# A twelve-layer decoder on one core: evacuations, divisions and norms change engines, and the first batch entry gets a queue of its own

## The chip, the cores and the metric

The kernel runs on one core of a Trainium2 chip, in one launch. The metric is the time of one execution in microseconds (us); the median of three runs of the kernel before is 2718.15 us. Engines are named as the profile names them: PE is TensorE (matrix products and transposes), DVE is VectorE, ACT is ScalarE, POOL is GpSimd and SP is SyncE, which issues the DMAs. PEld is the loading of weights into TensorE.

## The reference

The input is x with 4 batch entries, 512 positions and 128 features, and a context of 154 positions for each entry. Four groups of three layers follow, each added to its input and normalised:

```
x = norm(x + L0_attn(x));  x = norm(x + L0_xattn(ctx, x));  x = norm(x + L0_ffn(x))
x = norm(x + L1_attn(x));  x = norm(x + L1_xattn(x, ctx));  x = norm(x + L1_ffn(x))
x = norm(x + L2_attn(x));  x = norm(x + L2_xattn(x, ctx));  x = norm(x + L2_ffn(x))
x = norm(x + L3_attn(x));  x = norm(x + L3_xattn(x, ctx));  x = norm(x + L3_ffn(x))
```

L0_attn and L3_attn are self-attention with 16 heads of 8 features; L0_attn rotates x by position before it projects queries and keys with biases, L3_attn projects x down first. The four xattn layers are attention from the 512 positions to the 154 context positions, again 16 heads of 8; L0_xattn, L1_xattn and L2_xattn have biases on queries and keys, L3_xattn has none. L0_xattn puts the outputs of its heads back in another order and normalises twice, with a scale and an offset (gamma, beta) between. L1_attn is a state-space layer with a recurrence over the positions, L2_attn a causal attention with 16 heads of 64, and the ffn layers are gated or routed networks. All data are float32.

## The kernel before, in words

The order of work on every engine is written out by hand: each engine runs its instructions in the order in which the program emits them. A layer is a generator that yields between pieces, so that the end of a layer may be emitted among the first pieces of the next. An agenda holds small pieces of work for a later step.

**Operands in parts.** A head has only 8 features. To use TensorE's rows, and to keep float32 accuracy with bf16 products, queries and keys are split into three bf16 parts, and the parts are laid out so that one product of 64 rows gives a head's scores. `send` (L403) does this for one batch entry: a projection on TensorE (L407), its evacuation from PSUM to `raw` with scale and bias, on ScalarE where a scaled bias is at hand (L409, L411) and otherwise on VectorE (L413), four operations that cut `raw` into three parts (L414 to L417; cast, subtract, cast, subtract), and six DMAs that write the parts to a scratch in device memory, `far_q`, `far_k` or, for cross-attention, `far_kc` (L421). `arrive` (L479) loads the scratch back in the operands' layout with two DMAs into `qP` or `kP`. `other_rows` writes constant rows of the scratch at the start. The temporary `raw` and the parts come from a room that the layer gives (`room_to_send`), often with one buffer, so a second `send` waits for the first one's DMAs. All these DMAs are issued by SP.

**Maxima.** Scores are computed twice: once to reduce each row's maximum on VectorE, once transposed for the exponential on ScalarE. `split_maxima` (L493 to L496) turns the maxima into bf16 parts on GpSimd, and `link_maxima` turns these over on TensorE (L504) and adds them into rows of the query operand on VectorE (L506), so that the transposed product comes out with the maximum already subtracted.

**Self-attention** (`self_attention`) takes 64 steps, 16 for each batch entry. In a step come two score products (L667) and their maximum (L671) for a head pair six steps ahead, the transposed products (L683) and exponentials (L692) of this step, and the weighted sums (L706) of two steps back. Divisions by the sums, the output projection, the residual sum and the norm of a finished batch entry come from the agenda; `applied` (L344 to L346) is the norm's last operation, once for each of four tiles of 128 positions. In L0_attn `source` gives the rotated input: six operations on GpSimd (L789 to L794) and a transpose on TensorE. At steps 7, 10 and 13 of each 16, `new["room"]` lets the next layer send operands of its own ahead.

**Cross-attention** (`cross_attention`) goes in steps of four heads, 16 in all and two to fill the pipeline. In a step n: the first half of the scores and maxima (L949, L962) of step n+2 and of the transposed products (L957) and exponentials (L968) of step n; the first sums of step n-1 (L990); `link_maxima` for n+1; pieces of the agenda; the second halves; the remaining sums of n-1 (L999); the leftover keys of n (L978); `split_maxima` for n+2. In L0_xattn (`shuffled`) the remaining sums are followed on VectorE by a 32x32 transpose (L1011), a reciprocal (L1013) and the multiplication into `zt` (L1014). After four steps a batch entry's `zt` goes through `inner` (residual sum on GpSimd, L1025, and statistics on VectorE) and `outer` (`applied` on VectorE, then gamma, beta and residual on GpSimd, L1030 to L1032). What was not sent ahead is sent here: operands of entry b+2 after the second step of entry b.

**L2_attn** (`Causal`) normalises its probabilities on GpSimd (L1163), transposes them on TensorE (L1179) and copies them out on VectorE and ScalarE (L1515, L1526). During L1_attn and L2_attn, operands of the following cross-attention are sent.

Of the kernel before, what the change touches and what calls it, by code (L numbers as in the profile page):

```python
# [11 lines left out]
F32 = mybir.dt.float32  # L12
# [9 lines left out]
P = 128  # L22
# [152 lines left out]
def decoder_kernel(ctx: ExitStack, tc: tile.TileContext, x, ctxT, mask1, mask3, packs, offsets, out, layers):  # L175
# [102 lines left out]
    def other_rows(far, what, n):  # L278
        for r in range(2):
            nc.sync.dma_start(far[r, 48:, :, :], flat[:, what : what + 1, :n].to_broadcast([16, 8, n]))  # L280

# [61 lines left out]

    def applied(dst, ys, n, mv, rs):  # L344
        for t in range(n):
            nc.vector.tensor_scalar(  # L346
                dst[:, t, :], ys[:, t, :], mv[:, t, 0:1], rs[:, t : t + 1], ALU.subtract, ALU.mult
            )
# [42 lines left out]

    def scaled(what, scale, pool, name):
        if scale == 1.0:
            return what
        t = pool.tile([P, 1], F32, name=name, bufs=1)
        nc.vector.tensor_scalar(t, what, scale, None, ALU.mult)
        return t


    Q_ROWS, K_ROWS = ((0, 1, 3), (3, 2, 2), (4, 1, 1)), ((2, 1, 3), (1, 4, 2), (0, 1, 1))  # L400
    SLOT = 48

    def send(far, order, w, rhs, scale, bias, raw, part, scaled_bias=None, on=nc.gpsimd):  # L403

        n = rhs.shape[-1]
        pj = psum_t("ps_proj", kind="a" if "a" in ring else "t")
        nc.tensor.matmul(pj[:, :n], lhsT=w, rhs=rhs, start=True, stop=True)  # L407
        if bias is None:
            nc.scalar.activation(raw, pj[:, :n], AF.Copy, scale=scale)  # L409
        elif scaled_bias is not None:  # L410
            nc.scalar.activation(raw, pj[:, :n], AF.Identity, bias=scaled_bias, scale=scale)  # L411
        else:
            nc.vector.tensor_scalar(raw, pj[:, :n], bias, scale, ALU.add, ALU.mult)  # L413
        on.tensor_copy(part[:, 0, :], raw)  # L414
        on.tensor_tensor(raw, raw, part[:, 0, :], ALU.subtract)
        on.tensor_copy(part[:, 1, :], raw)
        on.tensor_tensor(part[:, 2, :], raw, part[:, 1, :], ALU.subtract)  # L417
        for i, (at, by, m) in enumerate(order):
            for r in range(2):
                rows = far[r].rearrange("(s k) p c -> (k p) s c", k=DK)  # L420
                nc.sync.dma_start(  # L421
                    rows[:, at : at + by * (m - 1) + 1 : by, :],
                    part[64 * r : 64 * r + 64, i : i + 1, :].to_broadcast([64, m, n]),
                )
# [41 lines left out]
    class Operands:  # L466
# [11 lines left out]

        def arrive(self, dst, far):  # L479

            for p in (slice(0, 2), slice(2, 8)):
                nc.sync.dma_start(dst[:, p, :], far.rearrange("r q p c -> (r q) p c")[:, p, :])

# [40 lines left out]

    def out_pieces(b, o, w, keep, cur, new, last, split=False):

        oT = keep.tile([P, S], F32, tag="oT", name="oT", bufs=1)
        ys = keep.tile([P, NT, D], F32, tag="ys", name="ys", bufs=1)
        xb = []

        def turn_over():
            pt = psum_a("ptO")
            for t in range(NT):
                nc.tensor.transpose(pt[:, t * P : (t + 1) * P], o[:, t].rearrange("p h d -> p (h d)"), ident)
            nc.scalar.copy(oT, pt)
            if "bo" in w:
                xb.append(with_bias(b, w["bo"], keep, cur))
            else:
                xb.append(cur["x"][:, b * NT : (b + 1) * NT, :])

        def times():
            yp = psum_a("yp")
            for t in range(NT):
                nc.tensor.matmul(
                    yp[:, t * P : (t + 1) * P], lhsT=oT[:, t * P : (t + 1) * P], rhs=w["wo"], start=True, stop=True
                )
            nc.vector.tensor_tensor(ys, yp.rearrange("p (t d) -> p t d", t=NT), xb[0], ALU.add)

        return [turn_over, times] + finish_pieces(b, ys, new, last, split)

    def finish_pieces(b, ys, new, last, split=False):
        xs = new["x"][:, b * NT : (b + 1) * NT, :]
        stats = []

        def norm():
            if split:
                applied(xs, ys, NT, *stats)
            else:
                normed(xs, ys, NT, "f")
            if last:  # L560
                nc.sync.dma_start(out[b].rearrange("(t p) d -> p t d", p=P), xs)
# [43 lines left out]
    def self_attention(w, source, q_scale, k_scale, room, keep, pool, cur, new, last):  # L605
# [4 lines left out]
        LEAD, LAG = 6, 2  # L610
        bqs = scaled(w["bq"], q_scale, pool, "bqs") if "bq" in w else None
        ops = Operands(pool, S, 2)
# [4 lines left out]
        def prepare(b):  # L617
# [21 lines left out]
            def queries():  # L639
                far = far_q[cur["index"] % 2][b]  # L640
                if ("q", b) not in cur["sent"]:
                    send(far, Q_ROWS, w["wq"], src, q_scale, bqs, *room_to_send(pool, S), scaled_bias=bqs)
                ops.arrive(m["q"], far)

            def keys():
                if ("k", b) not in cur["sent"]:

                    on = nc.vector if cur["index"] == 0 and b == 0 else nc.gpsimd
                    send(
                        far_k[b], K_ROWS, w["wk"], src, k_scale, w.get("bk"), *room_to_send(pool, S),  # L650
                        scaled_bias=w.get("bk"), on=on,
                    )
                ops.arrive(m["k"], far_k[b])
# [43 lines left out]
        def sums(s, h):  # L697
# [17 lines left out]
            if kt == NT - 1:  # L715
# [3 lines left out]
                if j == 3:  # L719
                    pieces = out_pieces(b, m["o"], w, keep, cur, new, last, split=True)  # L720
                    gaps = (2, 5, 6, 7, 10) if b < B - 1 else range(1, 6)
# [39 lines left out]
        for s in range(steps + LAG):  # L761
# [5 lines left out]

            new["room"] = (lambda n: room_to_send(pool, n)) if s % 16 in (7, 10, 13) else None
            yield PIECE
# [5 lines left out]
    def l0_attn(w, cur, new, last, room):  # L775
# [5 lines left out]
        def source(b):  # L781
# [4 lines left out]

            def turned():
                tmp = pool.tile([P, 2, NT, half], F32, tag="tmp", name="tmp", bufs=1)
                nc.gpsimd.tensor_tensor(rx[:, :, :half], x1, cos, ALU.mult)  # L789
                nc.gpsimd.tensor_tensor(rx[:, :, half:], x1, sin, ALU.mult)  # L790
                nc.gpsimd.tensor_tensor(tmp[:, 0], x2, sin, ALU.mult)
                nc.gpsimd.tensor_tensor(tmp[:, 1], x2, cos, ALU.mult)
                nc.gpsimd.tensor_tensor(rx[:, :, :half], rx[:, :, :half], tmp[:, 0], ALU.subtract)
                nc.gpsimd.tensor_tensor(rx[:, :, half:], rx[:, :, half:], tmp[:, 1], ALU.add)  # L794

# [19 lines left out]
    def cross_attention(w, cur, new, last, room, scale, mask=None, shuffled=False):  # L815
# [179 lines left out]
        def more_sums(n):  # L995
# [7 lines left out]
            if not shuffled:  # L1003
# [9 lines left out]
            nc.vector.reciprocal(rec, ot[:, :, DK])  # L1013
            nc.vector.tensor_tensor(  # L1014
                m["zt"][:, j, :].rearrange("p (s d) -> p s d", d=DK), ot[:, :, :DK],
                rec[:, :, None].to_broadcast([P, 16, DK]), ALU.mult,
            )
            if j == 3:
# [9 lines left out]
                def outer():  # L1028
                    applied(ys, zt, NT, *stats)
                    nc.gpsimd.tensor_tensor(ys, ys, w["gamma"][:, None, :].to_broadcast([P, NT, D]), ALU.mult)  # L1030
# [1374 lines left out]
```

## Time and profile before

| what | us |
|---|---|
| median of three runs (2717.45 to 2719.22) | 2718.15 |
| the profiled execution | 2717.01 |
| its span | 2715.2 |
| TensorE busy | 2445.9 |
| VectorE busy | 1705.6 |
| ScalarE busy | 1240.4 |
| GpSimd busy | 1043.7 |

The span is the time from the first to the last instruction of the profiled execution. Busy time counts instructions at work; a busy TensorE is not TensorE at its peak, since ends of matmuls are modelled. The stages that the change touches lie as follows in the span: the start of L0_attn from 0 to 33 us, its steps to 247, L0_xattn from 247 to some 368, the scans of L1_attn up to 842, L1_xattn from 850 to 1000, L2_attn around 1495 to 1850, L2_xattn from 1890 to 1970, L3_attn from 2100 to 2307, and L3_xattn after it.

In a timeline a line begins with the start and the duration of a group of like instructions in us, then engine, line of the program, operation, the tile written and those read, the shapes and the count. Square brackets give the idle time of the engine just before, and what ended it. "SPq" is SP's issuing of a DMA, not its transfer.

### The profile page before, as it was taken

How to read it: one execution, taken by the hardware profiler on the slowest of the kernel's cores; microseconds unless marked ns; L12 is line 12 of the kernel's file. 1: busy time of each engine (PE TensorE's matmuls, PEld its weight loads, DVE VectorE, ACT ScalarE, POOL GpSimd, SP SyncE). 2: the span in 40 equal slices, each digit the busy share in tenths (PEclk: the TensorE clock that was granted, in tenths of full speed). 3: DMA queues.
4: the chain of work that ended last, by engine and by line, in shares of the span. 5: the costliest groups of instructions: out<-in, count | busy, mean ns of one | idle time of the engine just before them, and what ended most of it. 6: DMA issues, size and time to landing. Idle time of an engine off the chain costs nothing. (4 is left out here: it accounts for less than half of the span.)

```text
span 2715.2 us, 37944 instructions
## 1 busy us (share of the span) xinstructions
PE 2445.9 (90%) x14378; PEld 1182.6 (44%) x14378; DVE 1705.6 (63%) x2931; ACT 1240.4 (46%) x2509; POOL 1043.7 (38%) x1360
## 2 busy tenths in 40 slices
PE   4897889978877989999999999998988999899998
PEld 1333334433334444444444555554455233446665
DVE  5896951289987665555545555556756887664444
ACT  2775432377642434333233555553543777343221
POOL 3332420167665327555542444443445332320000
PEclk9999999989988999999999999998987899999999
DMA  4422210000002400000000000002102241300000
GB/s 136 133 78 90 69 35 0 0 0 0 1 15 73 148 7 0 1 1 1 1 1 1 15 7 7 13 13 83 39 1 59 75 115 25 129 32 0 5 4 8
DMA packets 75558, 96.39 MB, mean 36 GB/s; under 512 B 23664, under 2 KB 62320, under 8 KB 75376
## 3 DMA queue, kind: packets, MB, share of 16 engines
q1 hardware_dynamic: 75376, 93.98, 11.8%
q8 instruction: 113, 1.85, 0.3%
q14 instruction: 69, 0.57, 0.1%
HBM read 63.92 MB, written 33.49 MB: 36 GB/s over the span
## 5 line engine op out<-in xcount | busy, mean ns | idle before, releaser
L1163 POOL TENSOR_TENSOR pr<-pr,zs 128x1024 f32<-128x1024 f32 x192 | 237.1, 1252 | 235.2 <-DVE zs L1160 204.8
L671 DVE TENSOR_REDUCE top<-sc 128x2 f32<-128x1024 f32 x256 | 300.9, 1215 | 37.7 <-PE sc L667 34.6
L692 ACT ACTIVATE pT<-st 128x512 f32<-128x512 f32 x512 | 275.9, 597 | 97.9 <-PE st L683 95.2
L1154 ACT ACTIVATE pr<-scc,nm 128x256 f32<-128x256 f32 (+3 forms) x384 | 198.3, 526 | 175.0 <-DVE nm L1148 107.0
L1148 DVE TENSOR_REDUCE nm<-scc 128x2 f32<-128x1024 f32 x192 | 153.6, 820 | 155.2 <-PE scc L1136 154.0
L962 DVE TENSOR_REDUCE top<-scx 128x4 f32<-128x616 f32 x256 | 192.1, 793 | 80.3 <-PE scx L949 77.3
L968 ACT ACTIVATE pTx<-stx 128x512 f32<-128x512 f32 x256 | 139.4, 596 | 206.8 <-PE scx L949 140.0
L2136 POOL TENSOR_TENSOR hh<-hh,cs 128x1024 f32<-128x1024 f32 x64 | 149.2, 2353 | 84.5 <-DVE hh L2132 61.0
L1287 DVE TENSOR_TENSOR vtmp<-psve,gm 128x1024 f32<-128x1024 f32 x64 | 78.3, 1224 | 153.0 <-PE psve L1282 59.6
L706 PE MATMUL av<-pT,vbuf 128*32 128x256 f32 x2048 | 162.6, 392 | 7.2 <-ACT avs L510 7.2
L493 POOL CAST nmP<-top 128x16 bf16<-128x16 f32 x96 | 25.8, 268 | 372.7 <-DVE top L962 214.3
L337 POOL TENSOR_TENSOR rsf<-mvf,eps 128x4 f32<-128x4 f32 x48 | 9.8, 204 | 392.8 <-DVE mvf L335 391.9
L1130 PE MATMUL scc<-k,q 64*128 64x512 f32 (+3 forms) x768 | 143.4, 471 | 6.7 <-ACT pr L1154 2.9
L2132 DVE TENSOR_TENSOR_SCAN hh<-da,pb 128x1024 f32<-128x1024 f32 x64 | 142.6, 2269 | 0.0
L1179 PE MATMUL ptc<-ident,pr 128*128 128x128 f32 x960 | 136.8, 280 | 5.7 <-POOL pr L1163 4.1
L667 PE MATMUL sc<-kP,qP 64*128 64x512 bf16 x512 | 106.2, 413 | 37.6 <-DMA kP<-far_k 18.9
L1292 POOL TENSOR_TENSOR vtmp<-vtmp 128x512 f32<-128x512 f32 x60 | 76.2, 1269 | 162.3 <-DVE vtmp L1287 137.8
L2145 PE MATMUL acc<-hh,ident 128*128 128x512 f32 x256 | 134.4, 652 | 1.9 <-DVE yt L2154 1.9
L1282 PE MATMUL psve<-w_L_ffn,xT 128*128 128x512 f32 x256 | 122.7, 603 | 14.4 <-ACT pr L1154 11.2
L1192 PE MATMUL avc<-pT,v 128*64 128x512 f32 (+3 forms) x768 | 131.4, 449 | 0.5 <-DVE pT L1515 0.5
L1325 PE MATMUL yT<-gT,w_L_ffn 128*128 128x512 f32 x256 | 123.2, 604 | 0.0
L1179 PEld LDWEIGHTS ptc<-ident,pr 128*128 128x128 f32 x960 | 103.4, 141 | 44.4 <-issue 26.0
(408 smaller groups left out, 5050.3 us busy)
## 6 DMA issues: line engine op xcount, KB each, us to landing
qP<-far_q SPq DMA_DIRECT2D x24, 768.0 KB, 6.1
w_L_ffn<-in_L_ffn SPq DMA_DIRECT2D x24, 512.0 KB, 8.5
far_q<-part SPq DMA_DIRECT2D x44, 192.0 KB, 2.8
qP<-far_q SPq DMA_DIRECT2D x24, 256.0 KB, 3.8
kP<-far_k SPq DMA_DIRECT2D x8, 768.0 KB, 5.8
far_q<-part SPq DMA_DIRECT2D x44, 128.0 KB, 2.4
kP<-far_kc SPq DMA_DIRECT2D x16, 231.0 KB, 4.8
w_L_attn<-in_L_attn SPq DMA_DIRECT2D x6, 512.0 KB, 6.5
```

The costliest lines, as they stand in the source:

```text
L671: return lambda: nc.vector.tensor_reduce(top[:, qt, 2 * gp : 2 * gp + 2], sc, AX.X, ALU.max, negate=True)
L692: nc.scalar.activation(pT, st, AF.Exp)
L706: nc.tensor.matmul(m["av"][32 * g : 32 * g + 32, part], lhsT=m["v"][:, kt, 4 * j + g, :], rhs=weights_of[s, g][:, part], start=(kt == 0 an ...
L962: nc.vector.tensor_reduce(ops.maxima(a)[:, 2 * qp : 2 * qp + 2, 2 * gp : 2 * gp + 2].rearrange("p i r -> p r i"), sc, AX.X, ALU.max, negat ...
L968: nc.scalar.activation(pT, st, AF.Exp)
L1130: nc.tensor.matmul(sc[:, r, at : at + n], lhsT=q[rows, qt * P : n], rhs=k[rows, :n], start=(i == 0), stop=False, skip_group_check=True,)
L1148: nc.vector.tensor_reduce(nm[:, i, :], sc[:, :, at : at + (qt + 1) * P], AX.X, ALU.max, negate=True)
L1154: nc.scalar.activation(pr[:, r, at:to], sc[:, r, at:to], AF.Exp, bias=nm[:, i, r : r + 1], accum_out=zs[:, i, r : r + 1],)
L1163: nc.gpsimd.tensor_tensor(pr[:, :, at : at + n], pr[:, :, at : at + n], zs[:, i, :, None].to_broadcast([P, 2, n]), ALU.mult)
L1179: nc.tensor.transpose(pt[:, r, to : to + P], self.pr[u, p][:, r, lo : lo + P], ident)
L2132: nc.vector.tensor_tensor_scan(flat, das[g % 2][:, c].rearrange("p n t -> p (n t)"), pbs[c].rearrange("p n t -> p (n t)"), 0.0, ALU.mult, ...
L2136: nc.gpsimd.tensor_tensor(m["h", j][c], m["h", j][c], m["C", j], ALU.mult)
```

## The change

- In `send`, the evacuation of every biased projection is a ScalarE activation. Where the scale isn't 1, one small VectorE operation scales the bias first. VectorE's evacuation (L413) is gone.
- For the first batch entry of L0_attn, the rotation and the split of the queries are on VectorE; the keys' `send` and `arrive` are issued from ScalarE's queue, and their temporaries come from a pool of their own, `first`.
- The norm's `applied` is on GpSimd for the first three batch entries of L0_attn and L3_attn, and in `outer` of L0_xattn.
- The multiplication into `zt` in L0_xattn is on GpSimd.
- `new["room"]` is given only up to step 59, so that the sends of step 61 come later, in the cross-attention after its second step.
- The order of the parts in the operands (`Q_ROWS`, `K_ROWS`, `SLOT`) is another one, of the same sizes.

```diff
@@ other_rows
-            nc.sync.dma_start(far[r, 48:, :, :], flat[:, what : what + 1, :n].to_broadcast([16, 8, n]))
+            nc.sync.dma_start(far[r, 32:48, :, :], flat[:, what : what + 1, :n].to_broadcast([16, 8, n]))
@@ applied
-    def applied(dst, ys, n, mv, rs):
+    def applied(dst, ys, n, mv, rs, on=nc.vector):
         for t in range(n):
-            nc.vector.tensor_scalar(
+            on.tensor_scalar(
                 dst[:, t, :], ys[:, t, :], mv[:, t, 0:1], rs[:, t : t + 1], ALU.subtract, ALU.mult
             )
@@ send
-    Q_ROWS, K_ROWS = ((0, 1, 3), (3, 2, 2), (4, 1, 1)), ((2, 1, 3), (1, 4, 2), (0, 1, 1))
-    SLOT = 48
-
-    def send(far, order, w, rhs, scale, bias, raw, part, scaled_bias=None, on=nc.gpsimd):
+    Q_ROWS, K_ROWS = ((1, 1, 3), (6, 1, 2), (0, 1, 1)), ((0, 3, 3), (1, 6, 2), (2, 1, 1))
+    SLOT = 32
+
+    def send(far, order, w, rhs, scale, bias, raw, part, on=nc.gpsimd, by=nc.sync):
...
-        elif scaled_bias is not None:
-            nc.scalar.activation(raw, pj[:, :n], AF.Identity, bias=scaled_bias, scale=scale)
         else:
-            nc.vector.tensor_scalar(raw, pj[:, :n], bias, scale, ALU.add, ALU.mult)
+            if scale != 1.0:
+                scaled_bias = small.tile([P, 1], F32, tag="sb", name="sb", bufs=2)
+                nc.vector.tensor_scalar(scaled_bias, bias, scale, None, ALU.mult)
+                bias = scaled_bias
+            nc.scalar.activation(raw, pj[:, :n], AF.Identity, bias=bias, scale=scale)
...
-                nc.sync.dma_start(
+                by.dma_start(
@@ arrive
-        def arrive(self, dst, far):
+        def arrive(self, dst, far, by=nc.sync):
...
-                nc.sync.dma_start(dst[:, p, :], far.rearrange("r q p c -> (r q) p c")[:, p, :])
+                by.dma_start(dst[:, p, :], far.rearrange("r q p c -> (r q) p c")[:, p, :])
@@ out_pieces and finish_pieces hand `on` through
-                applied(xs, ys, NT, *stats)
+                applied(xs, ys, NT, *stats, on=on)
@@ self_attention
-                    send(far, Q_ROWS, w["wq"], src, q_scale, bqs, *room_to_send(pool, S), scaled_bias=bqs)
+                    on = nc.vector if cur["index"] == 0 and b == 0 else nc.gpsimd
+                    send(far, Q_ROWS, w["wq"], src, q_scale, w.get("bq"), *room_to_send(pool, S), on=on)
...
             def keys():
+                if cur["index"] == 0 and b == 0:
+
+                    with tc.tile_pool(name="first", bufs=1, side="right") as first:
+                        send(
+                            far_k[b], K_ROWS, w["wk"], src, k_scale, w.get("bk"), *room_to_send(first, S),
+                            on=nc.vector, by=nc.scalar,
+                        )
+                    ops.arrive(m["k"], far_k[b], by=nc.scalar)
+                    return
...
-                    pieces = out_pieces(b, m["o"], w, keep, cur, new, last, split=True)
+                    on = nc.gpsimd if b < B - 1 else nc.vector
+                    pieces = out_pieces(b, m["o"], w, keep, cur, new, last, split=True, on=on)
...
-            new["room"] = (lambda n: room_to_send(pool, n)) if s % 16 in (7, 10, 13) else None
+            new["room"] = (lambda n: room_to_send(pool, n)) if s % 16 in (7, 10, 13) and s < 60 else None
@@ l0_attn, source
             def turned():
+                on = nc.gpsimd if b else nc.vector
...
-                nc.gpsimd.tensor_tensor(rx[:, :, :half], x1, cos, ALU.mult)
+                on.tensor_tensor(rx[:, :, :half], x1, cos, ALU.mult)
...
@@ cross_attention, more_sums
-            nc.vector.tensor_tensor(
+            nc.gpsimd.tensor_tensor(
                 m["zt"][:, j, :].rearrange("p (s d) -> p s d", d=DK), ot[:, :, :DK],
                 rec[:, :, None].to_broadcast([P, 16, DK]), ALU.mult,
             )
...
-                    applied(ys, zt, NT, *stats)
+                    applied(ys, zt, NT, *stats, on=nc.gpsimd)
```

## The prediction

> **What bounds the kernel now.** I read the page first (busy shares, chain), then the timeline stage by stage on the engines that the edits touch, since one edit meets six stages with different limits. 0.2% of this kernel is 5.4 us; less than that counts as no change.
>
> ```profile
> span 2715.2 us, 37944 instructions
> PE 2445.9 (90%) x14378; PEld 1182.6 (44%) x14378; DVE 1705.6 (63%) x2931; ACT 1240.4 (46%) x2509; POOL 1043.7 (38%) x1360
> PE 35%; DVE 6%; ACT 3%; POOL 2%; issue 1%; DMA 1%; SPq 0%; POOLq 0%; DVEq 0%; ACTq 0%
> ```
>
> TensorE carries the chain on average, so work taken off VectorE pays only where VectorE is what TensorE waits for. The first such place is the start, where nothing overlaps:
>
> ```profile
> 14.71 4.41 SPq L421 DMA_DIRECT2D far_q<-part  x6
> 20.78 0.83 SPq L482 DMA_DIRECT2D qP<-far_q  x2
> 21.66 4.24 SPq L421 DMA_DIRECT2D far_k<-part  x6
> 29.19 0.80 SPq L482 DMA_DIRECT2D kP<-far_k  x2
> ...
> 20.90 0.43 DVE L414 CAST part<-raw 128x512 bf16<-128x512 f32 x1 [14.55 <-DMA far_q<-part]
> ...
> 32.49 1.04 PE L667 MATMUL sc<-kP,qP 64*128 64x512 bf16 x4 [17.50 <-DMA kP<-far_k]
> ```
>
> The keys' split idles 14.55 us for the queries' sends (both used one buffer), and the first score matmul at 32.49 waits for the keys. The second place is the hand-over from L0_attn to L0_xattn:
>
> ```profile
> 242.22 4.68 SPq L421 DMA_DIRECT2D far_q<-part  x6
> ...
> 248.64 0.80 SPq L482 DMA_DIRECT2D kP<-far_kc  x2
> ...
> 254.46 0.69 PE L949 MATMUL scx<-kP,qP 64*128 64x154 bf16 x8 [6.12 <-DMA qP<-far_q]
> ```
>
> The loads issued at 248.64 stand behind the sends of the third query block. Third, L0_xattn, where VectorE is busy 42.6 of the 45 us from 300 to 345. One plain step of it, VectorE and then GpSimd:
>
> ```profile
> 283.42 0.70 DVE L1011 STREAM_TRANSPOSE ot<-avx 128x512 f32<-128x512 f32 x1
> 284.15 0.25 DVE L1013 RECIPROCAL recx<-ot 128x16 f32<-128x16 f32 x1
> 284.44 0.29 DVE L1014 TENSOR_TENSOR zt<-ot,recx 128x128 f32<-128x128 f32 x1
> 284.65 1.50 DVE L962 TENSOR_REDUCE top<-scx 128x4 f32<-128x616 f32 x2
> 286.07 0.68 DVE L506 TENSOR_TENSOR qP<-qP,pmx 128x1024 bf16<-128x1024 bf16 x1
> 286.66 1.50 DVE L962 TENSOR_REDUCE top<-scx 128x4 f32<-128x616 f32 x2
> ...
> 283.56 0.25 POOL L493 CAST nmP<-top 128x16 bf16<-128x16 f32 x1 [4.38 <-DVE top L962]
> 284.52 0.34 POOL L496 TENSOR_TENSOR nmP<-top,nmP 128x16 bf16<-128x16 f32 x1
> ```
>
> GpSimd turns the maxima into parts from 283.56 to 284.86, TensorE turns them over (0.62), and VectorE adds them (L506) at 286.07: they are some 0.3 us early. Last, L2_attn, where TensorE is full and GpSimd's order decides:
>
> ```profile
> 1625.02 1.02 ACT L1526 COPY pT<-ptc 128x1024 f32<-128x1024 f32 x1
> ...
> 1628.16 1.15 POOL L417 TENSOR_TENSOR part<-raw,part 128x512 bf16<-128x512 f32 x1
> 1629.28 3.03 POOL L1163 TENSOR_TENSOR pr<-pr,zs 128x768 f32<-128x768 f32 x3
> ...
> 1631.37 0.66 PE L1179 MATMUL ptc<-ident,pr 128*128 128x128 f32 x4 [0.72 <-POOL pr L1163]
> 1632.36 0.44 PE L1179 MATMUL ptc<-ident,pr 128*128 128x128 f32 x2 [0.34 <-POOL pr L1163]
> ```
>
> A query split already pushes the division of the probabilities back and costs TensorE 1.06 us, three times in the stage.
>
> **The change part by part.** The profiled execution took 2717.01 us (span 2715.2, 1.8 outside it); the median of the runs is 2718.15, 1.14 above. I sum against the former and carry that 1.14.
>
> **1. The first batch entry.** The rotation, six GpSimd operations of 0.72 (0.68 apart, 5.24 to 9.36), goes to VectorE, where a two-input operation of 1024 columns takes 1.2 and one of 512 takes 0.69: 0.35 to 0.5 each, done about 7.4, so 1.9 earlier, and so are the turn, projection and evacuation (raw at 12.1). The query split takes 2.3 on VectorE (row of the key split: 0.43, 0.69, 0.43, 0.69) instead of 3.7, done 14.4; the key split follows at once, done 16.7 instead of 23.2. The keys' six sends and two loads leave SP for ScalarE's queue: 0.7 apart, 14.9 to 18.6. In the built program query sends and key sends share completion counters: the second send of each query part waits for a key part to land. With 2.9 us to land (median row of these sends), SP issues the last query send near 20.5, it lands near 23, and two loads (0.8, then 3.7) end at 27 to 28. First scores near 27.5: **-5**. Bounds: -8 if the counters never bind, -3 if transfers slow each other as in the 5.7 us that key sends took before. Behind the key loads on ScalarE stand only exponentials that need these keys. Moving memory fills of GpSimd forward hides in its idle time.
>
> **2. The third query block** (two matmuls 1.12, evacuation, split 3.7, six sends 4.68) leaves step 61 of L0_attn and of L3_attn and passes, on SP, the eight loads of the cross-attention's first operands and, on GpSimd, their fills and four maxima splits. The loads then wait only for the last sums: 246.93 less 1.06 of TensorE instead of 248.64, **-2.7**; in L3, 2305.96 less 1.06 instead of 2307.19, **-2.2**. Bounds -3 and -1.1 each (only TensorE's share). In L0_xattn the new place costs TensorE time that it has (2.4 of 32 us idle around it), and GpSimd's 3.7 end just as the next division is ready; in L3_xattn TensorE is near full: **+1** (0 to 1.2).
>
> **3. L0_xattn, divisions and norms on GpSimd.** In GpSimd's order the division stands ahead of the maxima of the same step, and behind it wait the maxima, TensorE's turn, VectorE's add and the next reductions. Count from the start of the transpose, T. Division ready T+1.08 (0.73 + 0.29 + a hand-over of 0.06); on GpSimd about 0.46 (the nearest two-input 128x128 row, L1294: 0.458; from 0.29, its cast-like row, to 0.6); maxima split 1.30, ending T+2.9; turn 0.62 and hand-overs 0.09: add at T+3.6. Before it came at T+2.65. So a plain step grows 4.66 to 5.6. Step by step, with what VectorE loses (division 0.21, norm 1.1 to 1.7, one evacuation 0.66):
> - steps 1 to 3: 3 x 0.96 = +2.9;
> - steps 4 and 8: the inner statistics wait for GpSimd's residual sum (behind split 2.9, 0.85 and 1.27: T+5.1 instead of T+3.5): 2 x 1.6 = +3.2;
> - steps 5 and 6: VectorE sheds evacuation and norm (-1.4), but GpSimd has a query split (3.7), four norm operations (1.5 to 2.1) and three of 1.2 ahead of the next division, so the add of step 6 comes at T+8 instead of T+4.2: +2.3 together;
> - steps 9 and 10: -0.2 and 0; 7, 11, 12: +0.5, +0.6, +1.0; 13 to the end: +0.8.
> Sum **+11**. The norm's operation (one input, two per-partition scalars) has no GpSimd row: between a cast (0.29) and the slow little power operation L338 (1.02); I take 0.4, nearer the casts. At 1.02 three places grow by 4 x 0.6 = 2.4 each, and a 0.6 division adds 13 x 0.14 = 1.8: +20; the low end, all at 0.29, is +8.
>
> Row: VectorE's division, 0.21 start to start, against GpSimd's 0.458. The Trainium skill, "GPSIMD Engine Reference", section "Engine selection", advises VectorE for elementwise work, GpSimd being about twice as slow with two inputs; by twice the 0.29 the division would take 0.58 and the stage +12.5. "Perfetto Trace Analysis", section "Optimizing Scalar/DVE Operations", warns that the two engines share an SBUF read port, so moving between them may not help; the trace shows such a case (the division at 308.37 took 1.36 beside GpSimd's L1032). By that rule the moved work gives back no VectorE time, the -1.4 goes, and the sum is +12.4.
>
> **4. Biased evacuations on ScalarE** (VectorE 0.75 or 0.37 each; ScalarE 0.69 or about 0.4; a 0.15 scaling of the bias stays on VectorE).
> - L0_attn: seven, with three norms (12 x 0.34), leave VectorE: 6.9 us, but TensorE waits for maxima only 6.4 us in the stage: **-2.5** (0 to -6). The norms' new place on GpSimd is three steps ahead of use.
> - L1_attn: VectorE, bound by its scans, idles for the projection (2.8, 2.0, 1.4); without it, it starts when the earlier L2104 matmuls end, but ScalarE's decays now queue behind the evacuation: 0.6 + 0.8 + 0.6 = **-2** (0 to -3.5).
> - L1_xattn: the query evacuation's 1.95 wait for the key split moves to ScalarE; TensorE idles only 2.7 of 100 us here: **-0.8** (0 to -2.7).
> - L2_attn: the evacuation now stands behind ScalarE's copy 1625.02 to 1626.04, so the query split starts 1.1 later, and the probabilities and TensorE with it: 3 x 1.1 = 3.3. Key splits start 1503.5 instead of 1502.23; TensorE had 0.57 of slack there, 4 x 0.65 = 2.6. **+5.9** (3.3, only the queries, to 7).
> - L2_xattn: 0, TensorE is busy 39 of 40 us. L3_attn norms: **-0.5** (+0.5 to -2).
>
> The renumbered rows of the operands keep sizes and counts: nothing.
>
> Sum: -5 -2.7 -2.2 +1 +11 -2.5 -2 -0.8 +5.9 -0.5 = **+2.2**: 2719.2 for the profiled execution, 2720.4 as a median.
>
> **Rivals.**
> - *Cover holds in L0_xattn* (0.25): the late maxima meet slack that I don't see, and the stage breaks even: -11, 2709.4. For it: VectorE idles 3.9 of the 32 us from 268; against: the plain steps leave 0.3 us.
> - *GpSimd is dearer than its rows* (0.25), the other side: norms at 1.02 put L0_xattn at +18, and a start gated to -3 adds 2: 2729.4. It decides once a division plus a norm cost 3 us more over the stage than I took. For it: the 1.02 row and the blocked 1.36; against: 0.458 for the same shape.
> - *The later split hides in L2_attn* (inside the forecast's share): without that loss 2714.5, still no change. Against it: the 0.72 and 0.34 that TensorE already waits.
>
> **How the numbers follow.** Near-cancellation has 0.5 (of it 0.36 within 5.4 us, 0.14 slower), the first rival 0.25 (0.22 faster, 0.03 same), the second 0.25 (0.22 slower, 0.03 same): faster 0.22, same 0.42, slower 0.36. The bounds' deviations, added as squares, give -7 and +10; reaching to the rivals 2709 to 2731, where the likeliest alone is 2714 to 2728.
>
> **What would show it.** First score matmul near 27.5; loads of L0_xattn right after the last sums; the spacing of transposes in its plain steps 5.6 with TensorE's turn waiting for the maxima parts; GpSimd's 128x128 division near 0.46; in L2_attn the wait for the probabilities near 2.1 per query send. Wrong if the plain step stays at 4.7, if the norm costs 1 us an operation, or if query sends start only after all keys have landed.

## The result, and the profile after

The kernel changed takes 2719.18 us (median of 20 runs) against 2718.47 us for the kernel before (20 runs beside it). The ratio is 1.0005, with a 95% interval from 0.9997 to 1.0013: no change that can be told. The profiled execution has a span of 2718.2 us.

The busy times of the kernel changed, from its page:

```profile
PE 2445.7 (90%) x14378; PEld 1179.3 (43%) x14378; DVE 1681.6 (62%) x2872; ACT 1251.3 (46%) x2533; POOL 1071.5 (39%) x1406
```

VectorE lost 24 us of work, GpSimd gained 28, and the span stands where it was. To see where time went, I matched like instructions of both profiled executions and took the difference of their start times, after less before. The table gives how much each stretch added to that difference; the last column is the best kernel of this study, which is described below.

| stretch | forecast | changed | best |
|---|---|---|---|
| start, to 93 us | -5 | -3.2 | -2.9 |
| 93 to 111 | 0 | +3.3 | -5.8 |
| rest of L0_attn | -2.5 | -2.1 | -2.0 |
| hand-over to L0_xattn | -2.7 | -2.7 | -2.3 |
| L0_xattn, to 358 | +11 | +10.9 | -1.7 |
| 358 to the end of L1_attn | -2 | -10.0 | -9.2 |
| L1_xattn | -0.8 | +1.0 | +0.5 |
| 975 to 1480 (L1_ffn) | 0 | -0.1 | -2.6 |
| L2_attn, to 1870 | +5.9 | +8.3 | +0.1 |
| L2_xattn to 2108 | 0 | -1.4 | -1.6 |
| L3_attn | -0.5 | -1.8 | -1.5 |
| hand-over to L3_xattn | -2.2 | -1.3 | -0.9 |
| L3_xattn | +1 | +2.2 | +0.9 |
| after it | 0 | -0.3 | -2.0 |

The total was forecast well, but by errors of opposite sign: 3.3 us lost at 93 to 111 us and 2.4 more than forecast in L2_attn stand against L1_attn, which gained five times what I gave it. A row is one execution against one. Where other kernels of this study run the same code in a stretch, their profiles say how far it holds: the rest of L0_attn adds -2.0 in every one, L0_xattn with the division ahead of the maxima +9 to +11, the stretch from 688 to 858 -10.1 to -11.5; but the start adds -1.2 to -3.7, and 93 to 111 anything from -0.3 to +3.3. The stages one by one follow, each from the timeline of the kernel changed unless said otherwise.

**The start.**

```profile
14.51 7.45 SPq L416 DMA_DIRECT2D far_q<-part  x6
15.03 4.31 ACTq L416 DMA_DIRECT2D far_k<-part  x6
22.00 0.84 ACTq L477 DMA_DIRECT2D kP<-far_k  x2
23.56 0.83 SPq L477 DMA_DIRECT2D qP<-far_q  x2
29.01 1.03 PE L666 MATMUL sc<-kP,qP 64*128 64x512 bf16 x4 [15.74 <-DMA qP<-far_q]
```

The keys' loads are now issued at 22.00 instead of 29.19. The queries come last: SP takes 7.45 us for six sends instead of 4.41, since the second one waits for a key part to land; no other send waits for a key part. SP's wait (us in total, times, the longest):

```profile
SPq L416 <- DMA far_k<-part: 3.4, 1, 3.4
```

It issues the loads at 23.56. The first score is 3.5 us earlier than before; in ten profiles with this code it comes between 29.0 and 31.5, in the three with the old one between 32.5 and 33.8.

**93 to 111.** The next batch entry's rotated input is late in both kernels. Before:

```profile
94.97 0.31 POOL L414 CAST part<-raw 128x154 bf16<-128x154 f32 x1 [4.74 <-DMA far_kc<-part]
100.88 0.66 PE L354 MATMUL pt<-ident,rx 128*128 128x128 f32 x4 [4.10 <-POOL rx L794]
```

After:

```profile
94.01 0.31 POOL L409 CAST part<-raw 128x154 bf16<-128x154 f32 x1 [6.99 <-DMA far_kc<-part]
99.93 1.11 PE L354 MATMUL pt<-ident,rx 128*128 128x128 f32 x4 [6.37 <-POOL rx L795]
```

GpSimd's cast writes the one `part` tile that all sends share, and waits for the transfers out of it; the rotation stands behind it on GpSimd. TensorE arrived earlier and waited longer, and its matmuls then took 1.11 instead of 0.66: the granted clock from 93 to 112 is 0.73, before 0.91. The cast is only 0.96 us earlier than before, though the six sends that it waits for began 2.8 us earlier (86.86 instead of 89.69): the last of them, issued at 90.14, took twice as long to land (one send, so the three figures agree).

```profile
DMA to landing us min/median/max: 3.8/3.8/3.8
```

Before, the last send landed after 1.9 us. The run with the start undone, below, comes back to this.

**The hand-over to L0_xattn** is as forecast: the loads follow the last sums, and the first score comes at 249.65 instead of 254.46, 4.8 us earlier, of which 2.2 had been gained ahead of it.

```profile
244.92 0.80 SPq L477 DMA_DIRECT2D kP<-far_kc  x2
249.65 0.70 PE L950 MATMUL scx<-kP,qP 64*128 64x154 bf16 x8 [3.47 <-issue]
```

**L0_xattn.** One plain step, on VectorE, GpSimd and TensorE:

```profile
278.57 0.70 DVE L1012 STREAM_TRANSPOSE ot<-avx 128x512 f32<-128x512 f32 x1
279.31 0.25 DVE L1014 RECIPROCAL recx<-ot 128x16 f32<-128x16 f32 x1
...
279.64 0.41 POOL L1015 TENSOR_TENSOR zt<-ot,recx 128x128 f32<-128x128 f32 x1 [1.30 <-DVE recx L1014]
280.00 0.25 POOL L488 CAST nmP<-top 128x16 bf16<-128x16 f32 x1
...
281.28 0.62 PE L499 MATMUL pmx<-identb,nmP 128*128 128x128 bf16 x8 [0.88 <-POOL nmP L491]
281.94 0.69 DVE L501 TENSOR_TENSOR qP<-qP,pmx 128x1024 bf16<-128x1024 bf16 x1 [1.02 <-PE pmx L499]
...
283.95 0.70 DVE L1012 STREAM_TRANSPOSE ot<-avx 128x512 f32<-128x512 f32 x1
```

GpSimd stands idle 1.30 us for the reciprocal, divides, and only then turns to maxima that had been ready; TensorE waits for their parts, VectorE for TensorE. The step takes 5.39 us (283.95 less 278.57), before 4.66. TensorE's wait for `nmP` in the stretch 275 to 356 (us in total, times, the longest), before and after:

```profile
PE pmx L504 <- POOL nmP L496: 3.4, 2, 1.7
...
PE pmx L499 <- POOL nmP L491: 16.3, 11, 6.4
```

The groups of the moved operations, with the mean time of one in ns behind the busy time:

```profile
L346 POOL TENSOR_SCALAR ys<-zt,mvi,rsi 128x128 f32<-128x128 f32 x16 | 12.5, 793 | 0.1
L1015 POOL TENSOR_TENSOR zt<-ot,recx 128x128 f32<-128x128 f32 x16 | 6.5, 406 | 28.0 <-DVE recx L1014 28.0
```

**L1_attn.** What VectorE waited for from 783 to 836 us (us in total, times, the longest), before:

```profile
DVE pb L2129 <- PE pb L2104: 4.1, 3, 1.5
DVE sq L413 <- issue: 3.4, 2, 2.0
DVE sq L413 <- PE ps_proj L407: 2.8, 1, 2.8
```

After:

```profile
DVE x L346 <- POOL rsf L338: 1.6, 1, 1.6
DVE pb L2130 <- PE pb L2105: 1.2, 1, 1.2
```

Without the evacuations VectorE goes from scan to scan. The waits for the projection (6.2 us) are gone, and so are two of the three for `pb` that I had not put down to the evacuations.

**L2_attn.** The sending of one query block:

```profile
1624.22 1.02 ACT L1527 COPY pT<-ptc 128x1024 f32<-128x1024 f32 x1
1625.11 0.72 ACT L408 ACTIVATE raw<-ps_proj,sb 128x512 f32<-128x512 f32 x1
1625.90 0.61 POOL L409 CAST part<-raw 128x512 bf16<-128x512 f32 x1 [1.47 <-ACT raw L408]
1629.61 3.03 POOL L1164 TENSOR_TENSOR pr<-pr,zs 128x768 f32<-128x768 f32 x3
1631.70 0.66 PE L1180 MATMUL ptc<-ident,pr 128*128 128x128 f32 x4 [1.85 <-POOL pr L1164]
1632.70 0.44 PE L1180 MATMUL ptc<-ident,pr 128*128 128x128 f32 x2 [0.34 <-POOL pr L1164]
```

The evacuation stands behind ScalarE's copy, the split behind that, and TensorE waits 2.19 us (1.85 and 0.34) where it waited 1.06. Over the stage its waits for the probabilities grew from 4.1 us in eight waits to this:

```profile
PE ptc L1180 <- POOL pr L1164: 8.9, 12, 1.9
```

At the second query block more was lost. TensorE's busy time and granted clock there (the clock is the first figure behind the count), before:

```profile
1730.00:1735.00 5.00, 4.22 (x24) 1.00 0.07 15
1735.00:1740.00 5.00, 4.94 (x36) 1.00 0.02 5
```

After:

```profile
1734.00:1737.00 3.00, 3.00 (x7) 0.50 0.00 0
```

Behind a wait of 1.86 us the clock was 0.50, and the four projections that follow took 3.04 us instead of 1.88, the scores 1.62 instead of 1.14: 1.64 us that no count of waits shows.

### The profile page after: what moved, and what is told of

It is laid out like the page before. It is cut to its first block, busy times and chain, and to the rows that moved or that the text cites. A ratio compares the mean times of both kernels' runs of the same rounds, so it can differ in the third digit from the quotient of the medians.

```text
span 2718.2 us, 38015 instructions
## 1 busy us (share of the span) xinstructions
PE 2445.7 (90%) x14378; PEld 1179.3 (43%) x14378; DVE 1681.6 (62%) x2872; ACT 1251.3 (46%) x2533; POOL 1071.5 (39%) x1406
## 3 DMA queue, kind: packets, MB, share of 16 engines
q8 instruction: 113, 1.85, 0.3%
## 5 line engine op out<-in xcount | busy, mean ns | idle before, releaser
L1283 PE MATMUL psve<-w_L_ffn,xT 128*128 128x512 f32 x256 | 123.1, 605 | 14.5 <-ACT pr L1155 11.2
```

## The experiments

Differences of start times are given against the profiled execution of the kernel before. Each kernel's ratio is to the runs of the kernel before on the same chip; the kernel changed stands at 1.0005.

**The division behind the maxima.** The division stays on GpSimd, but is issued after the step's maxima split.

```diff
@@ more_sums
-            nc.gpsimd.tensor_tensor(
+            divisions.append(lambda: nc.gpsimd.tensor_tensor(
...
@@ step, after the maxima of step n+2
                 ops.split_maxima(a)
+            while divisions:
+                divisions.pop(0)()
```

> The changed kernel, with the GpSimd division of L0_xattn issued behind the split of the maxima of the same step instead of ahead of it; engine and work stay the same. Theory (place in GpSimd's queue): the maxima start right after the last reduction again, the plain step falls from 5.39 us to 4.5 to 4.7, some twelve steps by 0.7 give -8: about 2711. Rival (GpSimd is too dear, or its operations hold up VectorE's): the order makes no difference, the plain step stays above 5.2 and the time within 2 us of 2719.

Measured: 2709.57 us, ratio 0.9963 (0.9951 to 0.9975).

```profile
283.10 0.71 DVE L1012 STREAM_TRANSPOSE ot<-avx 128x512 f32<-128x512 f32 x1
283.25 0.26 POOL L488 CAST nmP<-top 128x16 bf16<-128x16 f32 x1 [2.87 <-DVE top L963]
284.40 0.40 POOL L1015 TENSOR_TENSOR zt<-ot,recx 128x128 f32<-128x128 f32 x1
...
287.54 0.71 DVE L1012 STREAM_TRANSPOSE ot<-avx 128x512 f32<-128x512 f32 x1
```

The division costs the same 0.40, but the maxima go first, and the step takes 4.44 us, 0.2 less than before the change. From 261 to 358 us the stage adds 0.8 us instead of 10.9. So the loss in L0_xattn was the division's place in GpSimd's order; its price on that engine cost the stage nothing.

**Division and norm back on VectorE.**

```diff
@@ more_sums
-            nc.gpsimd.tensor_tensor(
+            nc.vector.tensor_tensor(
@@ outer
-                    applied(ys, zt, NT, *stats, on=nc.gpsimd)
+                    applied(ys, zt, NT, *stats)
```

> The changed kernel, with divisions and norms of L0_xattn on VectorE as before. Theory: the stage's loss of 12 us (from 5.7 ahead at 276 us to 6.4 behind at 368) goes, plain steps are 4.66 again: about 2707. What it has over the division behind the maxima is the price of the norms on GpSimd. Rival: the loss in the stage comes from the third query block that is now sent there; then at most half of it goes, 2713 or more.

Measured: 2707.91 us, ratio 0.9957 (0.994 to 0.9974). The stage adds 1.2 us, as much as in the run above within what two profiles tell. The norms on GpSimd show only in where it is lost: with them the difference grows by 3.1 between 303 and 312 us and falls by 0.6 from there to 358; on VectorE it is -0.1 and +2.3.

**L2_attn's evacuations back on VectorE.** One branch in `send`, taken while the named layer sends ahead:

```diff
@@ send
+        elif evac["vector"]:
+            nc.vector.tensor_scalar(raw, pj[:, :n], bias, scale, ALU.add, ALU.mult)
         else:
...
@@ the driver, where a layer sends operands ahead
+                evac["vector"] = name in ('L2_attn',)
                 f(room)
+                evac["vector"] = False
```

> The changed kernel, with the evacuations that are sent during L2_attn on VectorE as before. Theory: GpSimd's splits start 1.1 to 1.5 us earlier, TensorE's wait for probabilities in the stage falls from 8.9 to 4.1 us, with the slower clock after the longest wait the stage regains 8: about 2711. Rival: the stage's loss is the ScalarE work itself or the later place in the clock's course, and the time stays within 3 us of 2719.

Measured: 2709.34 us, ratio 0.9967 (0.9956 to 0.9977). TensorE's waits for the probabilities are back to those of before, and its clock from 1725 to 1745 us is 1.00:

```profile
PE ptc L1184 <- POOL pr L1168: 4.1, 8, 0.7
```

From 1480 to 1870 us the stage adds 0.5 us. Over the kernels of this study that leave these evacuations on ScalarE it adds 7.8 to 11.0 us, over those with VectorE 0.1 to 0.5, whatever the rest of the kernel was.

**L1_attn's evacuations back on VectorE.** The same branch, for `'L1_attn'`.

> The changed kernel, with the evacuations that are sent during L1_attn on VectorE as before. Theory: VectorE waits for three projections again and for the broadcasts behind them, and the 10.5 us that the two profiles differ by between 780 and 835 us go: about 2729. Rival (the forecast's own working): only the waits for the projections themselves count, 2 us: 2721.

Measured: 2731.16 us, ratio 1.0046 (1.0031 to 1.0061), 11 us above the kernel changed. From 688 to 858 us the difference grows by 0.5 where in the kernel changed it falls by 11.2, and VectorE's waits are those of before to the tenth:

```profile
DVE pb L2134 <- PE pb L2109: 4.1, 3, 1.5
DVE sq L406 <- issue: 3.4, 2, 2.0
DVE sq L406 <- PE ps_proj L402: 2.8, 1, 2.8
```

So three waits for `pb` belong to the evacuations as well. That VectorE, once held up by a projection, also hands its next scan's result to GpSimd and TensorE late, and so meets a late `pb`, is my reading of the order; no run isolates it.

**Both gains together.** VectorE takes division, norm and L2_attn's evacuations.

> The two undone parts that gained (division and norm back on VectorE in L0_xattn; the evacuations sent during L2_attn on VectorE), together. Theory, that they are separate losses in stages that follow each other: the gains add, -10.6 and -9.2 against the 2718.5 of the kernel changed, so about 2699, a ratio of 0.993; the start times of VectorE's adds lie 7 us ahead of before at 339, 12 at 858, still 12 at 1870. Rival, that L2_attn gives back what an earlier start brings (it waits for something with a time of its own): 2706 to 2708, and the lead shrinks between 975 and 1870.

Measured: 2699.62 us, ratio 0.9928 (0.9916 to 0.9941). They add: 11.9 us ahead at 858, 11.3 at 1870.

**The start undone.** The first batch entry as before the change, all else changed.

```diff
@@ self_attention, queries
-                    on = nc.vector if cur["index"] == 0 and b == 0 else nc.gpsimd
+                    on = nc.gpsimd
@@ keys: the branch for the first entry is left out
-                    send(far_k[b], K_ROWS, w["wk"], src, k_scale, w.get("bk"), *room_to_send(pool, S))
+                    on = nc.vector if cur["index"] == 0 and b == 0 else nc.gpsimd
+                    send(far_k[b], K_ROWS, w["wk"], src, k_scale, w.get("bk"), *room_to_send(pool, S), on=on)
@@ turned
-                on = nc.gpsimd if b else nc.vector
+                on = nc.gpsimd
```

> The whole change but its first part: rotation and query split of the first batch entry on GpSimd, its keys sent from SP with the shared temporaries, as before. Theory, that the gain of the start is swallowed by a wait between 93 and 111 us (TensorE waits there for the rotated input from GpSimd, whose cast waits for the transfers of the context's keys): first score near 32.5, the wait for rx back near 4, and the time from 111 on within 2 us of the kernel changed, 2717 to 2721. Rival, that the start's 3.5 us reach the end: 2722.5, with start times 3.5 us later from 111 on than in the kernel changed.

Measured: 2721.27 us, ratio 1.0009 (1.0 to 1.0018). The first score comes at 32.92; TensorE waits 3.6 us for the rotated input instead of 6.4, and at 111 us the difference is -0.2, in the kernel changed +0.1. In these two profiles, what the start gained was gone there. The total lies between the two expectations, and the intervals of the two ratios overlap, so the totals can't tell a difference of 3 us.

That the wait takes the gain as such doesn't hold against the other profiles. With L1_attn's evacuations on VectorE the code up to 234 us is that of the kernel changed, and the last send, issued at 89.49, landed, and TensorE waited, like this:

```profile
DMA to landing us min/median/max: 1.9/1.9/1.9
...
97.38 0.91 PE L354 MATMUL pt<-ident,rx 128*128 128x128 f32 x4 [4.26 <-POOL rx L799]
```

There the whole gain passes. All profiles in which the context's keys share the tile, with the difference to before:

| first batch entry | last send landed after | at 93 us | at 111 us |
|---|---|---|---|
| old: before; this run | 1.9 | 0; +0.5 | 0; -0.2 |
| new: L1_attn's evacuations, or division and norm, on VectorE | 1.9 | -3.7; -1.2 | -3.5; -1.5 |
| new: the kernel changed and four others | 3.2 to 3.8 | -3.2 to -2.2 | +0.1 to +1.2 |
| new, but the keys on SP (next run) | 3.8 | +0.3 | +3.0 |

At like landing the new start is ahead at 111 us, by 1.3 to 3.5 us. The 3 us or so that are lost at 93 to 111 go with the late landing, 1.3 to 1.9 us of it and the slower clock behind the longer wait. What makes the send land late isn't shown: it did in six of eight profiles with the changed first entry and in neither of the two without, too few to tie it to the change.

**The keys on SP.** The changed start, but with the keys' sends and loads issued by SP.

```diff
-                            on=nc.vector, by=nc.scalar,
+                            on=nc.vector,
...
-                    ops.arrive(m["k"], far_k[b], by=nc.scalar)
+                    ops.arrive(m["k"], far_k[b])
```

> The change with the first keys' sends and loads issued by SP behind the queries', and their own room and VectorE's split kept. Theory, that the queue of its own is what the start gains beyond the 2 us of the faster rotation: key sends start only when SP has issued the query loads (near 19), 4.3 us of them and the loads behind, first score near 31. Rival, that the sends on two queues hold each other up (completion counters shared, landing 5 us): with one queue the queries land sooner and the first score comes at 29 or earlier. Total within 2 us of the kernel changed in both.

Measured: 2719.66 us, ratio 1.0008 (0.9998 to 1.0017).

```profile
20.62 0.83 SPq L477 DMA_DIRECT2D qP<-far_q  x2
21.50 4.35 SPq L416 DMA_DIRECT2D far_k<-part  x6
30.04 0.80 SPq L477 DMA_DIRECT2D kP<-far_k  x2
33.34 1.04 PE L666 MATMUL sc<-kP,qP 64*128 64x512 bf16 x4 [20.48 <-DMA kP<-far_k]
```

Both numbers missed: the first score is at 33.34, later even than before the change. On one queue the key loads follow the queries' loads, 4.2 us behind the last key send. So the queue of its own carries the whole gain of the start, and the faster rotation none that one profile shows. Against the kernel changed it is 4.3 us late at the first score, 3.0 at 111 and still 2.2 at 2293; at the end it is 0.9 ahead. That comes from code that the two kernels share: from 2340 to 2600 us the kernel changed and two others add 0.1 us, this one and nine more -1.5 to -1.6.

**The third query block early.** `and s < 60` left out of the condition of `new["room"]`.

> The change with the third query block sent at step 61 of L0_attn and L3_attn again. Theory, that its sends on SP delay the loads of the cross-attention's first operands: the first score of L0_xattn comes 2.7 us later and that of L3_xattn 1.3 later than in the kernel changed, L3_xattn itself is up to 2 us shorter, L0_xattn 0 to 2 shorter: 2719 to 2722. Rival, that the block's new place in L0_xattn costs as much as the hand-over gains or more (its split stands ahead of a division on GpSimd there): L0_xattn at least 4 us shorter and 2715 or less.

Measured: 2725.57 us, ratio 1.0029 (1.0018 to 1.0041), outside both. The hand-over to L0_xattn is 2.2 us dearer than in the kernel changed and the stage itself 1.0 longer, so the block's later place costs nothing there. The rest comes from a place where both kernels have the same code, in L1_xattn:

```profile
926.92 1.04 PE L499 MATMUL pmx<-identb,nmP 128*128 128x128 bf16 x8 [2.83 <-POOL nmP L491]
927.75 2.02 PE L539 MATMUL yp<-w_L_xattn,oT 128*128 128x128 f32 x8
```

The matmuls of the last line took 1.11 us in the kernel changed, after a wait of 0.61. The clock granted from 927 to 932 us is 0.50, and against the kernel changed 5.1 us are lost. GpSimd came late because a cast into a shared part tile began 6.2 us after its predecessor, in the kernel changed 4.0. It is the wait of 93 to 111 again: the last of the six sends out of that tile landed 3.3 us after its issue, in the kernel changed and all other profiles after 1.9 to 2.0. Why, and whether the other executions have it too, is not settled.

**Tiles of their own for the context's keys.** `raw` and `part` of the context keys sent during L0_attn are no longer those of the other sends.

```diff
+    def room_for_keys(pool):
+        raw = pool.tile([P, KC], F32, tag="raw_k", name="raw_k", bufs=2)
+        part = pool.tile([P, 3 * KC], BF16, tag="part_k", name="part_k", bufs=2)
+        return raw, part.rearrange("p (i n) -> p i n", i=3)
...
-            new["room"] = (lambda n: room_to_send(pool, n)) if s % 16 in (7, 10, 13) and s < 60 else None
+            new["room"] = (
+                lambda n: room_for_keys(pool) if n == KC and cur["index"] == 0 else room_to_send(pool, n)
+            ) if s % 16 in (7, 10, 13) and s < 60 else None
```

> The change, and the keys of the context that are sent ahead during L0_attn get raw and part tiles of their own, two of each, instead of one that all sends share. Theory, that the wait of TensorE between 93 and 111 us (6.4 us for the rotated input, behind a GpSimd cast that waits 7.0 for the transfers out of the shared tile) is what swallows the start's gain: without the shared tile the cast starts when its input is there, the wait falls below 2, TensorE keeps its clock there, and start times from 111 on are 4 to 6 us earlier than in the kernel changed: 2713 to 2715. Rival, that the cast's input or the next turn on GpSimd is as late anyway, or that VectorE sets the pace behind it: the wait stays above 4 or the time is back by 234, 2717 or more.

Measured: 2710.11 us, ratio 0.9962 (0.9947 to 0.9977).

```profile
86.06 0.31 POOL L409 CAST part_k<-raw_k 128x154 bf16<-128x154 f32 x1 [0.34 <-DMA far_kc<-flat]
...
92.99 0.66 PE L354 MATMUL pt<-ident,rx 128*128 128x128 f32 x4
```

The cast goes 8 us earlier, TensorE waits for nothing there, and at 111 us the kernel is 9.5 us ahead of before, more than the 4 to 6 expected: the wait of 6.4 and the slower matmuls behind it are both gone. That is not luck of the landing: here too the last send landed late, after 3.3 us, and no cast waits for it. Against the profile with the shared tile and the early landing (-3.5 at 111) it is 6 us.

**The best version.** The last edit on top of both gains together.

> The version with division, norm and the evacuations during L2_attn on VectorE, with the context keys' own tiles added. If the wait at 93 to 111 is a loss of its own: 2699.6 less 4 to 6, 2694 to 2696. If not: 2698 to 2701.

Measured: 2686.65 us (7 below the range expected), ratio 0.9877 (0.9861 to 0.9894): 33 us faster than the kernel before, and faster than the kernel changed. Of the 14.3 us between the profiles of this version and of both gains together, 9.6 stand at 111 us and at 234, 12.5 at 975 and 14.0 at 1100; what lies behind 234 is in code that the edit doesn't touch. The busy times:

```profile
PE 2427.3 (90%) x14358; PEld 1175.2 (44%) x14378; DVE 1697.3 (63%) x2908; ACT 1248.3 (47%) x2526; POOL 1054.3 (39%) x1374
```

TensorE is busy 18.6 us less than before with the same work (20 of its records are missing here); from 93 to 112 us its clock is 1.00, before 0.91. The mean clock of the whole execution, 0.968 against 0.959, doesn't make the time: the three other executions of this version had 0.960 to 0.962 and took as long.

**The start undone in the best version.**

> The best version so far (division, norm and the evacuations during L2_attn on VectorE, own tiles for the context keys) with the first batch entry's rotation, query split and key queue as before the change. Theory, that with the wait at 93 to 111 gone the start's gain is no longer swallowed: start times 3 to 4 us later than in that version at 93, at 234 and at the end, 2689.5 to 2691. Rival, that something later takes the start's gain away even so: 2687 or less, and the difference is gone by 234.

Measured: 2694.63 us, ratio 0.9913 (0.9896 to 0.9929), 8 us above the best and above the range of both expectations. It is 4.0 us later at 93 us and still 4.0 at 234: with the wait gone the start's gain passes on. A further 1.4 us is lost by 358, which is left open, and 2.3 between 1000 and 1100, in L1_ffn, which the start doesn't touch: there the best's clock stays at 1.00, in this profile it is 0.74 from 990 to 1000. The best's profile gains 2.3 us on before there; the others lie between 0.8 ahead and 1.2 behind.

**The third block early in L3_attn alone, in the best version.** The condition reads `(s < 60 or cur["index"] > 0)`.

> The best version so far, with the third query block sent at step 61 again in L3_attn alone. Theory, that its later place costs L3_xattn 2.3 us for the 1.3 of the hand-over: from 2293 to the end 1 us shorter, 2685.5 to 2686.5, which only the start times can tell. Rival, that the hand-over's gain is the larger: 1 us longer there or more, 2687.5.

Measured: 2688.77 us, ratio 0.9893 (0.9878 to 0.9907). From 2293 to the end it is 1.2 us longer than the best, while the earlier run with the early block is 1.0 shorter there than the kernel changed. The block's worth in L3 is within about 1 us of nothing, and its sign not settled.

## Why the prediction was right, and where its steps were wrong

The forecast was 2720.4, and 2719.18 was measured. The parts were off by up to 8 us, so that they cancel to within 1.2 us is in part luck.

- **Start, -5: mis-sized, and its way to the end was not followed.** The last query send was issued at 21.38 (forecast 20.5) and landed at 23.44 (23), but the first of the query loads took 5.4 us to land instead of 4.5 and the first score came at 29.0, so -3.5, close to the bound of -3. Of the three shared counters only the first held SP up. The larger error is that I let those microseconds count to the end. 60 us on stood a wait set by transfers out of a shared tile, already 4.1 us long in the profile of before; in the kernel changed its last send landed 1.9 us later, and 3.3 us were lost. In profiles where it landed early, 1.5 and 3.5 us of the start's gain are left at 111 us; with the wait gone, 4. One reading was off too: of the 14.55 us that VectorE idled ahead of the keys' split, only the last 2.4 were a wait for the queries' sends, since `raw` was ready at 18.54.
- **Third query block, -2.7 and -2.2, +1:** the first exact, the second -1.3, and L3_xattn +2.2 for +1.
- **L0_xattn, +11: right in sum and cause.** The plain step was forecast 5.6 and took 5.39. The division was cheaper than taken (0.41 for 0.46), the norm twice as dear (0.79 for 0.4); I had put that operation near the casts, when the slow power operation (1.02) was the closer row. The norm's price hardly reaches the stage's end. The weighing against the Trainium skill, "GPSIMD Engine Reference", section "Engine selection", comes out two ways: for its factor of two with two inputs the division shows 1.4 (0.41 on GpSimd, 0.29 in the median on VectorE before), while the norm, one input with two scalars a row, which by that section would be roughly as fast, took 0.79 against 0.34. The shared port of which "Perfetto Trace Analysis" warns was not varied in any run. The profile of before agrees with it: two of the sixteen divisions began 0.06 us behind GpSimd's L1032 (1.27 us), took 1.36 and ended 0.15 behind it; thirteen took 0.29.
- **L1_attn, -2: the step that failed.** I let VectorE's next start be set by TensorE and ScalarE at once, and left 4.1 us of waits for `pb` as they were. With three evacuations (1.5 us) and nine microseconds of waits gone the stage gained 10 to 11. That the evacuations cause it is shown by the run that puts them back; how they bring the waits for `pb` about is argued.
- **L2_attn, +5.9: right mechanism, short by 2.4.** The wait per query block was forecast near 2.1 and is 2.19. All waits for the probabilities grew by 4.8 us, so the key splits cost some 1.4, not 2.6. Missing were the slower clock behind one of these waits (1.64) and 1.2 at the stage's end.
- **L0_attn -2.5, L1_xattn -0.8, L3_attn -0.5** came at -2.1, +1.0 and -1.8.
- **The rivals.** "Cover holds in L0_xattn" fell: there was no slack. "The later split hides in L2_attn" fell with it. "GpSimd is dearer than its rows" was half true, of the norm alone, and didn't decide, since the order and not the price set the stage.

## What to carry to other kernels

An operation that changes engines is priced by its place in the new engine's order first: the same division cost 10 us in front of the maxima and none behind them. An early gain is followed to the next wait for a transfer or a shared buffer before it is added to a sum: here that wait grew by as much as the gain in five of seven profiles, and a buffer of its own removed it in all four that had one. A difference of 3 us between two single profiles is held against other profiles of the same code before a cause is read into it. Where an engine that bounds a stage blocks on a round trip through others, look for the second wait that the first one brings about: it goes too.

## What the runs showed of the hardware

TensorE's clock falls behind short waits, and not always. After 1.85 us of waiting at 1631 us the clock stayed at 1.00, after 1.86 us at 1731 it was 0.50 from 1734 to 1737; in the profile with the start undone it was 0.50 to 0.57 over 3 us behind all three of these waits. After 2.83 us in L1_xattn it was 0.50 for 5 us. The first of these slow places cost 1.64 us beside its wait; the one in L1_xattn 5.1, of which the longer wait is 2.2. The Trainium skill, "TensorE: Matmul & The Clock Gate", Part 1, tells of a half clock after an idle window of about 3.4 us, with a window that runs free of the program. The half clock and the chance agree with these runs, and so do the waits of 4.10 and 6.37 us at 93 to 111, behind which the clock fell too; but those of 1.86 and 2.83 us are shorter than that window.

The last of the six sends out of the shared tile at 93 to 111, 19.2 KB, landed after 1.9 us in four profiles and after 3.2 to 3.8 in six.

GpSimd took 0.79 us for a norm operation of 128x128 with two scalars a row, and 0.41 for a product of two inputs of that size.
